# Keys of elements 1 to 7: the seventh block product by a second level of Strassen, and the queries' evicted blocks in the large pool

## The chip, the cores and the metric

The kernel runs on one core of a Trainium2 chip, in one launch. The metric is the device time of that launch in microseconds (us). Its engines are written as in the profile: PE (the matmul engine) with PEld (its weight loads), DVE (vector), ACT (scalar), POOL (GpSimd, here a queue for accumulating DMAs) and SP (a queue for plain DMAs).

## The reference

Two attention layers run over a batch of 8 elements of 512 channels and 32x32 = 1024 tokens, all in float32. Cut to what matters:

```
# layer 0, for each element: x is [1024 tokens, 512]
xn = layer_norm(x) * gamma + beta
q, k, v = xn @ Wq.T + bq, xn @ Wk.T + bk, xn @ Wv.T + bv     # 8 heads of 64
x = softmax(q k^T / 8) v @ Wo.T + bo + x
# layer 1: x is [512, 1024]
h = group_norm(x); q, k, v = wq h + bq, wk h + bk, wv h + bv  # one head of 512
x = x + wp (v softmax(q^T k / sqrt(512))^T) + bp
```

The change touches the projection `k = xn @ Wk.T + bk` of layer 0 for elements 1 to 7, and where the projection `q` of the same elements keeps some evicted blocks.

## The kernel before

A 512x512 weight times a 512x1024 operand is computed as a two by two block product in Strassen's form (Winograd's variant): `STEPS` (line 54) lists seven products of a 256-row weight block or sum of blocks ("11", "12", "S1" to "S4", "22") and an operand block or sum ("11", "21", "22", "T1" to "T4"), with the PSUM bank that each goes to ("x", "y" or "z") and whether it opens that bank. The class `Product` (line 366) runs these steps one at a time: `multiply()` issues the matmuls of a step and `leave()` its eviction. After steps 0, 2 and 3 ACT copies a bank out (`copy`), after steps 1, 4 and 5 DVE adds such a copy and a bank (`out`), after step 6 ACT evicts the last block (`whole`).

For elements 1 to 7 the keys and queries of layer 0 go through `project_deep` (line 589). It takes six of the seven outer products to a second level: each is itself a seven-step `Product` of 128x128 blocks, whose operands are the "deep" sums of a block's quarters. They run as three tandems (`TANDEMS`, line 68), each tandem doing two outer products into the two halves of a bank, so a step is two matmuls of 128x128 weights and 256 columns. The first two tandems run step by step side by side, then the third runs alone. The seventh outer product, weight block "22" times operand "T4", is not taken to the second level: `plain(n)` (line 654) computes it with four matmuls of 128x128 weights and 512 columns, one behind each of the third tandem's steps 0, 1, 3 and 5, in the two banks of the PSUM tile `x0`, and ACT evicts each half with the bias into a tile `m6`. `last()` (line 675) adds `m6` to the other products. The deep sums of the weights were computed and written to DRAM in the first element (`save_deep_later`, line 225), three groups of two for the keys, and `load_deep` reads them back for each element. The deep sums of the operand are made by `deep_operands_later` on DVE, two queue entries for each operand.

What matters for the order: all engines but SP run in the order in which the code is written (`manual_schedule`). Small work is spread over the matmuls by a queue, `side`: `later(...)` appends entries, `tick(n)` pops and runs n of them, and a `Product` calls `tick(self.pieces)` between `multiply()` and `leave()` of each step. Tiles come from pools, in turn: `big` has 46 tiles of 128x1024, `half` 9 tiles of 128x512, PSUM has `ps_s`, 3 tiles of two banks (scores, `x0`, `x1`, `z`), and `ps_a`, two single banks (`bank(...)`).

Element 0 is different. While its queries are projected (lines 1724 to 1731), the queue gets the entries that make the keys' deep weight sums, then the layer norm of element 1 (`ln.queue()`); while its values are projected (from line 1735), the queue also has the deep sums of the other weights. The layer norm's entry puts itself back as second of the queue as long as it has more steps, so it takes turns with the other entries:

```
                    side.insert(len(side) if self.waiting == "now" else 1, piece)
```

Its `variance()` step takes a bank of `ps_a` for two matmuls (`over_channels`, line 1014), and the next step, the first of `root()`, reads that bank with a DVE transpose (line 959). After the values come the scores of the first two pairs of heads, one after the other and with no tick between (`next_scores`, line 1747). In `Pair.scores` (line 1253) block m of a pair is two matmuls of 64 rows that run side by side, mostly into the two banks of a `ps_s` tile that ACT evicts with one exponential; but for three blocks of every two pairs each matmul takes a bank of `ps_a` and has an exponential of its own:

```
                if m + self.c % 2 * NM in (7, 11, 15):
                    s = None
                    parts = [bank(f"s{i}_{self.tag}_{m}") for i in range(2)]
```

Those are block 7 of the first pair and blocks 3 and 7 of the second.

Of the kernel before, what the change touches and what calls it, by code (L numbers as in the profile page):

```python
# [12 lines left out]
F32 = mybir.dt.float32  # L13
I32 = mybir.dt.int32
AF = mybir.ActivationFunctionType
# [5 lines left out]
P = 128  # L21
# [50 lines left out]
def fast_path(ctx: ExitStack, tc: tile.TileContext, x: bass.AP, vecs: dict, weights: dict, out: bass.AP,  # L72
# [13 lines left out]
    nc = tc.nc  # L86
# [18 lines left out]
    def big_tile(name):  # L105
        return big.tile([P, S], F32, tag="b", name=name)

    def half_tile(name):
        return half.tile([P, HB], F32, tag="h", name=name)
# [4 lines left out]
    def bank(name):  # L114
        return ps_a.tile([P, HB], F32, tag="a", name=name)
# [93 lines left out]
            nc.sync.dma_start(out=t, in_=d)  # L209
        return w  # L210

    saved_deep = {n: dram.tile([P, 3, 2, 4, P], F32, tag=f"saved_deep_{n}", name=f"saved_deep_{n}") for n in ("k", "q", "a", "m")}

    def deep_tile(n, b, g):
        return big_tile(f"w_{n}_{b}_{g}_deep").rearrange("p (s i o) -> p s i o", s=2, i=4)

    def load_deep(n, b, groups=range(3), queue=nc.sync):
        ready = {}
        for g in groups:
            deep = deep_tile(n, b, g)  # L220
            queue.dma_start(out=deep, in_=saved_deep[n][:, g])
            ready.update({name: deep[:, k] for k, name in enumerate(SLOTS[2 * g : 2 * g + 2])})
        return ready

    def save_deep_later(n, w, groups=range(3)):

        def sums(g):
            left, right = w[g][:, :, :, :P], w[g][:, :, :, P:]
            made = []

            def one(i, l, r, op):
                if not made:
                    made.append(deep_tile(n, "first", g))
                d = made[0]
                l, r = (d[:, :, x] if isinstance(x, int) else x for x in (l, r))
                nc.vector.tensor_tensor(d[:, :, i], l, r, op)

            later(lambda: one(0, right[:, :, 0], right[:, :, 1], ALU.add),
                  lambda: one(2, left[:, :, 0], right[:, :, 0], ALU.subtract),
                  lambda: one(1, 0, left[:, :, 0], ALU.subtract),  # L240
                  lambda: one(3, left[:, :, 1], 1, ALU.subtract),
                  lambda: nc.gpsimd.dma_start(out=saved_deep[n][:, g], in_=made[0]))

        for g in groups:
            sums(g)
# [340 lines left out]
        for n in names:  # L586
            later(lambda n=n: first(n), lambda n=n: rest(n))

    def project_deep(tag, w, w_deep, bias, h, h_deep, pieces, early):


        made = [[None, None] for _ in TANDEMS]
        wides = {}
        res = {}

        def banks(to, j):
            if to == "y":
                return bank(f"y_{tag}_{j}")
            n = to if to == "z" or j == 2 else f"x{j}"
            if j == 2:  # L600
                return wides["z"][:, :HB] if to == "x" else wides["x1"][:, HB:]
            wides[n] = wides[n] if n in wides else wide_psum(f"{n}_{tag}")
            return wides[n][:, ts(j if to == "z" else 0, HB)]

        def part(dst, a, b, opens):
            for s in range(2):
                nc.tensor.matmul(dst[:, ts(s, CB)], a[s], b[s], start=(opens and s == 0), stop=True,  # L607
                                 skip_group_check=True)

        def view(t):  # L610
            return t.rearrange("p (s t) -> p s t", s=2)

        def unit(j):
            def dest(i, k):
                if made[j][i] is None:
                    made[j][i] = big_tile(f"{tag}_{j}{i}").rearrange("p (s t) -> p s t", s=2)
                return made[j][i][:, :, ts(k, CB)]

            def shift(u, ps, which, add=None):
                if j == 1:  # L620
                    nc.scalar.activation(u, ps, AF.Identity, bias=bias(which[0]))
                else:
                    nc.scalar.copy(u, ps)

            a, b = TANDEMS[j]
            u = Product(f"{tag}_{j}", weight_inner(w, w_deep, a), operand_inner(h, h_deep, b), part, shift, dest,
                        lambda to: banks(to, j))
            u.view = view
            if j < 2 and early:
                for i in range(2):  # L630
                    if j == 0:
                        wides["u", i] = big_tile(f"u{i}1_{tag}")
                    u.loaded[i, 1] = wides["u", i][:, ts(j, HB)]
            return u

        def add(dst, src):
            nc.gpsimd.dma_start(out=dst, in_=src, accum_op=ALU.add)

        def run():
            first, second, third = (unit(j) for j in range(3))  # L640
            for i in range(len(STEPS)):
                first.multiply()
                second.multiply()
                tick(pieces)
                first.leave()
                second.leave()
                yield
            t13, t27, t54 = made
            for r in range(2):
                add(t27[r][:, 0], t13[r][:, 0])  # L650
            until(lambda: "T4" in h)
            rest = {}

            def plain(n):
                r, k = divmod(n, 2)
                ps = wides["x0"]
                nc.tensor.matmul(ps[:, ts(r, HB)], w["22"][:, k, ts(r, P)], h["T4"][:, k, :], start=(k == 0),
                                 stop=(k == 1), skip_group_check=True)
                if k == 1:
                    u = rest[r] = half_tile(f"m6_{tag}_{r}")  # L660
                    nc.scalar.activation(u, ps[:, ts(r, HB)], AF.Identity, bias=bias(2 + r))

            for i in range(len(STEPS)):
                third.step()
                if i in (0, 1, 3, 5):
                    plain((0, 1, 3, 5).index(i))
                if i == 1:
                    for r in range(2):
                        nc.vector.tensor_add(t13[r][:, 1], t13[r][:, 1], t13[r][:, 0])
                        add(t27[r][:, 1], t13[r][:, 1])  # L670
                yield
            for r in range(2):
                add(t27[r][:, 1], t54[r][:, 1])

            def last():
                for r in range(2):
                    nc.vector.tensor_add(t54[r][:, 0], t54[r][:, 0], t13[r][:, 1])
                for r in range(2):
                    nc.vector.tensor_add(lower[r][:, 0], rest[r], t54[r][:, 0])
                for r in range(2):  # L680
                    nc.vector.scalar_tensor_tensor(lower[r][:, 1], t54[r][:, 1], bias(2 + r), t54[r][:, 0], ALU.add,
                                                   ALU.add)

            lower = [big_tile(f"{tag}_lower_{r}").rearrange("p (s t) -> p s t", s=2) for r in range(2)]
            for r in range(2):
                res[r], res[2 + r] = t27[r], lower[r]
            res["last"] = last
            yield
        return run(), res
# [973 lines left out]
    def bias_of(n):  # L1663
        return lambda oc: vec(n, oc)

    with tc.manual_schedule(engines=ORDERED):
# [56 lines left out]

        units, qt = project("q0", wq_now, bias_of("bq0"), hb)
        ln.xt = load_x(1)
        save_deep_later("k", wk_now)
        units[0].step(3)
        ln.queue()
        for u in units:
# [11 lines left out]
        for b in range(B):  # L1741
# [177 lines left out]
                u.finish()  # L1919
            if more:  # L1920
                wk_next = load_w("k", b + 1)
                wk_deep = load_deep("k", b + 1, queue=nc.scalar)
            for u in o_units:
                u.pieces = 2
            o_units[0].rest()
# [1 line left out]
            if not more:  # L1927
                o_units[1].step(1)
            if more:
                deep_operands_later(hb, h_deep, primes_of_h[2:])  # L1930
            o_units[1].rest()
            if more:
                wq_next = load_w("q", b + 1)
                wq_deep = load_deep("q", b + 1)
                steps, kt = project_deep(f"k{b + 1}", wk_next, wk_deep, bias_of("bk0"), hb, h_deep, 2, True)
                for _ in steps:
                    pass
                steps, qt = project_deep(f"q{b + 1}", wq_next, wq_deep, bias_of("bq0"), hb, h_deep, 1, False)
                for n, _ in enumerate(steps):
                    if n == 0:  # L1940
                        kt["last"]()
                    if n == 2 and ln:
                        ln.waiting = False
                qt["last"]()
                vts = {ik: big_tile(f"v{b + 1}_again_{ik[0]}{ik[1]}") for ik in vn_away}
                for ik, d in vn_away.items():
                    nc.sync.dma_start(out=vts[ik], in_=d)
# [384 lines left out]
```

## Time and profile before

| | |
|---|---|
| median of 4 runs | 2790.87 us (2790.64 to 2791.11) |
| the profiled execution | 2789.62 us, of which the span of the core's instructions is 2787.8 us |
| granted PE clock in it | 0.999 |
| busy: PE, PEld | 2777.1, 1628.7 us |
| busy: DVE, ACT, POOL | 2159.2, 1271.4, 521.6 us |
| keys and queries of element 1 in `project_deep` | 419 to 462.5 us of the span |
| first scores of element 0 | 122.66 to 136.66 us |

Busy times are unions of the instructions' spans. A float32 matmul of the program is two MATMUL rows in the trace. The 2789.62 us are 1.25 us under the median of the runs; the sum of the prediction is made as a difference to this execution and carried over to the median.

### The profile page before, as it was taken

The page shows a single profiled execution, that of the slowest core. Times are in us where ns is not written, and L with a number is a line of the kernel's source. Part 1 is how long each engine was busy: PE and PEld are TensorE (multiplying, and loading weights), DVE is VectorE, ACT ScalarE, POOL GpSimd, SP SyncE. Part 2 cuts the span into 40 slices and gives each one's busy share as a digit, 9 for nine tenths or more (in the row PEclk, how much of TensorE's full clock was granted, in tenths as well). Part 3 has the DMA queues.
Part 4 walks back from the last instruction along what each step waited for, and adds up shares of the span by engine and source line. Part 5 has one row for each costly group of instructions (what it writes and reads, how often), then busy time and mean ns, then how long its engine had stood idle before and what let it go on. Part 6 is the DMA issues. An engine that isn't in the chain of part 4 may idle for free.

```text
span 2787.8 us, 32637 instructions
## 1 busy us (share of the span) xinstructions
PE 2777.1 (100%) x11343; PEld 1628.7 (58%) x11343; DVE 2159.2 (77%) x3082; ACT 1271.4 (46%) x2138; POOL 521.6 (19%) x718
## 2 busy tenths in 40 slices
PE   9999999999999999999999999999999999999999
PEld 4535766357553685536854467644676347763375
DVE  6687897778867788777877778778887778857776
ACT  4463435724357242662436534365334743336342
POOL 2031022210222102221022211222012210122001
PEclk9999999999999999999999999999999999999999
DMA  8244467353763547536474364744547434282223
GB/s 317 91 116 126 125 154 193 69 148 102 186 165 70 164 113 195 123 78 186 110 197 102 92 185 114 203 79 113 161 116 208 99 98 132 61 211 63 67 91 96
DMA packets 142462, 370.86 MB, mean 133 GB/s; under 512 B 19936, under 2 KB 24336, under 8 KB 142288
## 3 DMA queue, kind: packets, MB, share of 16 engines
q0 software_dynamic: 58128, 141.08, 27.0%
q1 hardware_dynamic: 81040, 216.56, 22.1%
q10 hardware_dynamic: 3120, 11.04, 1.2%
q8 instruction: 92, 1.51, 0.2%
q14 instruction: 82, 0.67, 0.1%
HBM read 206.59 MB, written 64.49 MB: 97 GB/s over the span
## 4 chain that ended last, share of the span: by engine, by line
PE 99%; DMA 0%; DVE 0%; ACT 0%; issue 0%; SPq 0%; DVEq 0%
PE s L1263 16%; PE acc L1281 16%; PE x_o L509 8%; PE s L1429 7%; PE x_v L493 4%; PE y_o L509 4%; PE x_out L484 4%; PE y_s L1429 3%; PE y_v L493 2%; PE s L1464 2%; PE c_vm L827 2%; PE y_out L484 2%; PE z_o L509 2%; PE x_q L607 2%; PE x_k L607 2%; PE c_qa L701 2%
## 5 line engine op out<-in xcount | busy, mean ns | idle before, releaser
L1272 DVE TENSOR_TENSOR sum<-sum,p 128x1024 f32<-128x1024 f32 x384 | 470.3, 1225 | 40.1 <-ACT p L1266 1.4
L1266 ACT ACTIVATE p<-s 128x1024 f32<-128x1024 f32 (+1 forms) x608 | 478.8, 991 | 15.1 <-PE s L1263 15.1
L1281 PE MATMUL acc<-p,v_again 128*64 128x512 f32 x1792 | 390.9, 594 | 0.0
L1281 PEld LDWEIGHTS acc<-p,v_again 128*64 128x64 f32 x1792 | 126.1, 137 | 261.3 <-issue 236.7
L970 POOL DMA_DIRECT2D fold<-sum x312 | 207.1, 744 | 345.3 <-DMA sum<-sum 212.0
L1263 PE MATMUL s<-q,k 64*128 64x512 f32 x1152 | 252.1, 592 | 0.0
L1263 PE MATMUL s<-q_lower,k_lower 64*128 64x512 f32 x896 | 196.1, 592 | 0.0
L1270 DVE TENSOR_TENSOR sum<-p,p 128x1024 f32<-128x1024 f32 x64 | 78.1, 1220 | 149.4 <-ACT p L1266 149.4
L1263 PEld LDWEIGHTS s<-q,k 64*128 64x128 f32 x1152 | 109.7, 186 | 138.2 <-issue 85.0
L1263 PEld LDWEIGHTS s<-q_lower,k_lower 64*128 64x128 f32 x896 | 85.4, 186 | 110.5 <-issue 68.5
L974 POOL DMA_DIRECT2D sum<-sum x78 | 63.9, 845 | 415.5 <-DVE sum L1272 261.2
L1285 ACT COPY o<-acc 128x512 f32<-128x512 f32 x63 | 36.9, 585 | 221.7 <-PE acc L1281 221.5
L1469 DVE TENSOR_TENSOR p<-p,p 128x1024 f32<-128x1024 f32 x96 | 112.9, 1216 | 6.3 <-ACT p L514 6.3
L509 PE MATMUL x_o<-T_p,S_vm 128*128 128x512 f32 x256 | 114.0, 592 | 0.0
L514 ACT COPY u(0, 0)_v<-x_v 128x512 f32<-128x512 f32 x16 | 9.4, 585 | 186.5 <-PE x_v L493 186.5
L484 PE MATMUL x_out<-T_o,w_o 128*128 128x512 f32 x192 | 89.2, 594 | 0.0
L509 PEld LDWEIGHTS x_o<-T_p,S_vm 128*128 128x128 f32 x256 | 48.6, 190 | 60.8 <-issue 60.8
L1327 ACT COPY rr<-r 32x16 f32<-32x16 f32 x256 | 53.5, 209 | 62.0 <-DVE r L1230 58.6
L493 PE MATMUL x_v<-w_v,T_h 128*128 128x256 f32 x336 | 80.0, 381 | 0.0
L964 DVE STREAM_TRANSPOSE rden<-rr 128x512 f32<-128x512 f32 (+1 forms) x72 | 53.3, 757 | 22.5 <-ACT rr L1572 13.7
L493 PEld LDWEIGHTS x_v<-w_v,T_h 128*128 128x128 f32 x336 | 63.3, 190 | 11.3 <-issue 3.4
L1417 ACT ACTIVATE p<-p 128x1024 f32<-128x1024 f32 x64 | 65.3, 1061 | 0.0
(665 smaller groups left out, 5570.7 us busy)
## 6 DMA issues: line engine op xcount, KB each, us to landing
sum<-sum POOLq DMA_DIRECT2D x78, 256.0 KB, 3.4
fold<-sum POOLq DMA_DIRECT2D x312, 64.0 KB, 2.3
x<-in_x_dram SPq DMA_DIRECT2D x32, 512.0 KB, 6.6
xr<-in_x_dram SPq DMA_DIRECT2D x64, 256.0 KB, 4.2
x_away<-x SPq DMA_DIRECT2D x32, 512.0 KB, 2.8
v_away<-v SPq DMA_DIRECT2D x28, 512.0 KB, 3.0
v_again<-v_away SPq DMA_DIRECT2D x28, 512.0 KB, 9.0
w_o<-saved_o SPq DMA_DIRECT2D x24, 512.0 KB, 5.3
```

The costliest lines, as they stand in the source:

```text
L484: nc.tensor.matmul(dst, a[:, k, ts(r, P)], b[:, k, :], start=(opens and k == 0), stop=(k == 1), skip_group_check=True)
L493: nc.tensor.matmul(dst[:, ts(m, CB)], b[:, k, ts(2 * r + m, P)], a[:, k, :], start=(opens and m == 0 and k == 0), stop=(k == 1), skip_grou ...
L509: nc.tensor.matmul(dst, a[:, r, ts(m, P)], b[m // 2][:, m % 2, :], start=(opens and m == 0), stop=(m == NM // 2 - 1), skip_group_check=True)
L607: nc.tensor.matmul(dst[:, ts(s, CB)], a[s], b[s], start=(opens and s == 0), stop=True, skip_group_check=True)
L970: nc.gpsimd.dma_start(out=f[ts(q + i, BL), :], in_=t[ts(n, BL), ts(i, HB)], accum_op=ALU.add if n else ALU.bypass)
L1263: nc.tensor.matmul(parts[i], self.k[m // 4][r, ts(m % 4, P)], self.q[r, :], start=True, stop=True)
L1266: nc.scalar.activation(dst, src, AF.Exp, scale=1.0 / float(D) ** 0.5)
L1270: nc.vector.tensor_add(self.sum, self.p[0], p)
L1272: nc.vector.tensor_add(self.sum, self.sum, p)
L1281: nc.tensor.matmul(acc[i * D : (i + 1) * D, :], value_of(self.vt, m, self.c * P + i * D, D), self.p[m][:, ts(i, HB)], start=(m == 0), stop ...
L1429: nc.tensor.matmul(dst[:, ts(c, CB)], x[0][:, ts(c, P)], a[0], start=(opens and c == 0), stop=True, skip_group_check=True)
L1469: nc.vector.tensor_add(wide(t), wide(t), wide(x))
```

## The change

Keys: the seventh outer product becomes a `Product` of its own, `sixth`, of seven steps with one matmul of 128x128 weights and 256 columns each. It runs in step with the third tandem, in `x0` (bank "x"), the first bank of `x1` ("z") and a bank of `ps_a` ("y"). Its three copies go to a large tile `u6`, its results to the two tiles `m6`. For that the fourth group of deep weight sums (block "22") is made and saved in element 0 and loaded for each element, and "T4" gets deep sums too. Queries: still with `plain`, but the copies `u(0, 1)` and `u(1, 1)` of the first two tandems are kept in large tiles, as the keys' were (`early`).

```diff
-    saved_deep = {n: dram.tile([P, 3, 2, 4, P], F32, ...
+    saved_deep = {n: dram.tile([P, 4, 2, 4, P], F32, ...
     def load_deep(n, b, groups=range(3), queue=nc.sync):
...
+            names = SLOTS[2 * g : 2 * g + 2]
-            queue.dma_start(out=deep, in_=saved_deep[n][:, g])
+            queue.dma_start(out=deep[:, : len(names)], in_=saved_deep[n][:, g, : len(names)])
...
-    def project_deep(tag, w, w_deep, bias, h, h_deep, pieces, early):
+    def project_deep(tag, w, w_deep, bias, h, h_deep, pieces, early, deep_sixth):
...
+        def sixth_unit(rest):
+            def dest(i, k):
+                if i not in rest:
+                    rest[i] = half_tile(f"m6_{tag}_{i}")
+                return rest[i][:, ts(k, CB)]
+
+            def shift(u, ps, which, add=None):
+                nc.scalar.activation(u, ps, AF.Identity, bias=bias(2 + which[0]))
+
+            def bank_of(to):
+                return bank(f"y6_{tag}")[:, :CB] if to == "y" else wides["x0" if to == "x" else "x1"][:, :CB]
+
+            def narrow(dst, a, x, opens):
+                nc.tensor.matmul(dst, a[0], x[0], start=opens, stop=True, skip_group_check=True)
+
+            u = Product(f"{tag}_6", weight_inner(w, w_deep, ("22",)), operand_inner(h, h_deep, ("T4",)), narrow, shift,
+                        dest, bank_of)
+            u6 = big_tile(f"u6_{tag}")
+            u.loaded = {which: u6[:, ts(n, CB)] for n, which in enumerate(((0, 0), (0, 1), (1, 1)))}
+            return u
...
+            sixth = sixth_unit(rest) if deep_sixth else None
             for i in range(len(STEPS)):
-                third.step()
-                if i in (0, 1, 3, 5):
-                    plain((0, 1, 3, 5).index(i))
+                if sixth:
+                    third.multiply()
+                    sixth.multiply()
+                    tick()
+                    third.leave()
+                    sixth.leave()
+                else:
+                    third.step()
+                    if i in (0, 1, 3, 5):
+                        plain((0, 1, 3, 5).index(i))
...
-        save_deep_later("k", wk_now)
+        save_deep_later("k", wk_now, range(4))
...
-                wk_deep = load_deep("k", b + 1, queue=nc.scalar)
+                wk_deep = load_deep("k", b + 1, range(4), nc.scalar)
...
-                deep_operands_later(hb, h_deep, primes_of_h[2:])
+                deep_operands_later(hb, h_deep, primes_of_h[2:] + ["T4"])
...
-                steps, kt = project_deep(f"k{b + 1}", ..., hb, h_deep, 2, True)
+                steps, kt = project_deep(f"k{b + 1}", ..., hb, h_deep, 2, True, True)
-                steps, qt = project_deep(f"q{b + 1}", ..., hb, h_deep, 1, False)
+                steps, qt = project_deep(f"q{b + 1}", ..., hb, h_deep, 1, True, False)
```

`save_deep_later` makes the same four sums (on one block instead of two) and one store for the fourth group, so it appends five entries more to `side`.

More of the change, by code (lines that the diff above doesn't have):

```diff
@@ L210, in load_w @@
         return w
-    saved_deep = {n: dram.tile([P, 3, 2, 4, P], F32, tag=f"saved_deep_{n}", name=f"saved_deep_{n}") for n in ("k", "q", "a", "m")}
+    saved_deep = {n: dram.tile([P, 4, 2, 4, P], F32, tag=f"saved_deep_{n}", name=f"saved_deep_{n}") for n in ("k", "q", "a", "m")}
     def deep_tile(n, b, g):
@@ L219, in load_deep @@
         for g in groups:
+            names = SLOTS[2 * g : 2 * g + 2]
             deep = deep_tile(n, b, g)
-            queue.dma_start(out=deep, in_=saved_deep[n][:, g])
-            ready.update({name: deep[:, k] for k, name in enumerate(SLOTS[2 * g : 2 * g + 2])})
+            queue.dma_start(out=deep[:, : len(names)], in_=saved_deep[n][:, g, : len(names)])
+            ready.update({name: deep[:, k] for k, name in enumerate(names)})
         return ready
@@ L227, in sums @@
         def sums(g):
-            left, right = w[g][:, :, :, :P], w[g][:, :, :, P:]
+            s = len(SLOTS[2 * g : 2 * g + 2])
+            left, right = w[g][:, :s, :, :P], w[g][:, :s, :, P:]
             made = []
@@ L233, in one @@
                     made.append(deep_tile(n, "first", g))
-                d = made[0]
+                d = made[0][:, :s]
                 l, r = (d[:, :, x] if isinstance(x, int) else x for x in (l, r))
@@ L241, in sums @@
                   lambda: one(3, left[:, :, 1], 1, ALU.subtract),
-                  lambda: nc.gpsimd.dma_start(out=saved_deep[n][:, g], in_=made[0]))
+                  lambda: nc.gpsimd.dma_start(out=saved_deep[n][:, g, :s], in_=made[0][:, :s]))
         for g in groups:
@@ L1934, in fast_path @@
                 wq_deep = load_deep("q", b + 1)
-                steps, kt = project_deep(f"k{b + 1}", wk_next, wk_deep, bias_of("bk0"), hb, h_deep, 2, True)
+                steps, kt = project_deep(f"k{b + 1}", wk_next, wk_deep, bias_of("bk0"), hb, h_deep, 2, True, True)
                 for _ in steps:
                     pass
-                steps, qt = project_deep(f"q{b + 1}", wq_next, wq_deep, bias_of("bq0"), hb, h_deep, 1, False)
+                steps, qt = project_deep(f"q{b + 1}", wq_next, wq_deep, bias_of("bq0"), hb, h_deep, 1, True, False)
                 for n, _ in enumerate(steps):
```

## The prediction

> **What bounds the kernel now.** I read the page's busy times and the chain that ended last, then PE's waits, to see whether anything but PE's own work has a price.
>
> ```profile
> PE 2777.1 (100%) x11343; PEld 1628.7 (58%) x11343; DVE 2159.2 (77%) x3082; ACT 1271.4 (46%) x2138; POOL 521.6 (19%) x718
> PE 99%; DMA 0%; DVE 0%; ACT 0%; issue 0%; SPq 0%; DVEq 0%
> ```
>
> The waits of PE, complete:
>
> ```profile
> PE pst_k L304 <- DMA w_k<-in_L_conv_wk_dram: 1.9, 1, 1.9
> PE ps_first L1669 <- DVE checks L142: 1.3, 1, 1.3
> PE pm L1203 <- DVE mv L1197: 0.6, 1, 0.6
> PE x_qa L484 <- DVE gn L1225: 0.4, 1, 0.4
> PE psw_a L315 <- ACT nat_k L307: 0.2, 1, 0.2
> PE pst_q L304 <- DMA w_q<-in_L_conv_wq_dram: 0.2, 1, 0.2
> ```
>
> PE is the chain from end to end, and it waits 4.6 us in all, none of it in the stages the change touches. So a PE column taken away is time gained, a new PE wait is time lost, and nothing later can win it back. Three places decide. The first is PE's timeline at the start of the keys' third tandem (start, length, what; a length runs to the modelled end of the last matmul of the line):
>
> ```profile
> 431.38 1.03 PE L607 MATMUL z_k<-T_h,w_k 128*128 128x256 f32 x4
> 432.24 1.02 PE L657 MATMUL x_k<-T_h,w_k 128*128 128x512 f32 x2
> 433.10 1.03 PE L607 MATMUL x_k<-T_h,w_k 128*128 128x256 f32 x4
> 433.96 1.02 PE L657 MATMUL x_k<-T_h,w_k 128*128 128x512 f32 x2
> ```
>
> One plain matmul (two rows of 512 columns) holds PE for 433.10 - 432.24 = 0.86 us; a step of the tandem (two matmuls of 256 columns, four rows) also 0.86, so one narrow matmul takes 0.43. The second is ACT's timeline in the same stage, where two evictions must be out before PE may reuse their bank:
>
> ```profile
> 431.58 0.69 ACT L621 ACTIVATE k<-x_k,vecs 128x512 f32<-128x512 f32 x1 [0.28 <-PE x_k L607]
> 441.05 0.58 ACT L623 COPY k<-z_k 128x512 f32<-128x512 f32 x1 [0.17 <-PE z_k L607]
> ```
>
> The third is element 0: the layer norm's variance bank, its transpose, and the first scores. The lines are from the timelines of PE, DVE and ACT, the last one being ACT's answer for the instant about 130 us.
>
> ```profile
> 112.82 1.08 PE L1014 MATMUL var<-lnq,ones_c 128*64 128x512 f32 x4
> 113.97 0.72 DVE L959 STREAM_TRANSPOSE vart<-var 128x512 f32<-128x512 f32 x1 [0.29 <-PE var L1014]
> 122.66 14.00 PE L1263 MATMUL s<-q,k 64*128 64x512 f32 x64
> 123.84 14.96 ACT L1266 ACTIVATE p<-s 128x1024 f32<-128x1024 f32 x19 [0.48 <-PE s L1263]
> 129.28 1.57 ACT L1266 ACTIVATE p<-s 128x1024 f32<-128x1024 f32 x2
> ```
>
> Before, the bank is free 1.9 us after it was taken, and 8 us before the scores. The 16 score blocks then run without a break: 0.86 us each on PE, 0.90 on ACT, which falls slowly behind.
>
> **Part 1, the seventh product: a gain.** Removed for each element: 4 x 0.86 = 3.44 us of PE. Added: 7 x 0.43 = 3.03 (by the chain of waits, where eight rows of 256 columns take 1.73: 14 x 0.216). That is -0.41 an element, -2.9 us over seven. The Trainium skill's page "TensorE: Matmul & The Clock Gate", section "Back-to-back issue gap", speaks against it: it gives a sustained spacing of 81 ns for 128 columns and 131 ns for 512, so a narrow matmul would cost more for each column. Read off halfway, about 98 ns for 256 columns (an estimate from that page), eight wide rows would become 14 narrow ones at 1.05 against 1.37 us, and the part would lose 2.3 us. The trace has 0.43 and 0.216 us for the two widths, exactly proportional, and I go by it.
>
> **What is added beside PE, at nothing.** DVE: three deep sums of "T4" (0.68 + 0.42 + 0.42 by lines 577, 581 and 582) and three adds of 128x256 from PSUM; no row has that shape, 0.42 is the row of 128x256 in SBUF and 0.69 the row of 128x512 from PSUM, I take 0.42. Together 2.8 us an element. From 419 to 441 us DVE is busy 12.2 of 22 us, which covers it. ACT: four evictions of 128x256 in the place of two of 0.69; between nothing less than 0.3 and 0.69 each, I take 0.45, so +0.4 us, beside 8.8 busy of 22. One load more of 256 KB on ACT's queue, with one issue of 0.44 us at about 400 us, where ACT next sits idle 2.1 us. Its bytes share the DMA engines (281 GB/s from 419 to 441, so 0.9 us of them). Who would feel it is the queries' deep weights: last issued at 426.4, median landing 12.2, first used at 444.3, 5.7 us to spare. If all that cover were gone, each late microsecond there would cost one on PE. The queries' two copies in large tiles change an address and no instruction: nothing, between -0.1 and +0.1 an element, since ACT waits for no tile there.
>
> **Two covers get thinner.** Step 1 of the tandem waits for the ACT line at 431.58, out at 432.27. Its weight load must start one row before its matmul: 432.67 before, 432.46 with 0.43 in the place of 0.86. About 0.15 us is left with the semaphore's 0.04. At the end, the built order of the changed program lets the queries' second matmul wait for the k<-z_k copy: it is out 1.65 us after the last tandem step starts, and the weight load comes 0.86 + 0.43 + 0.86 - 0.22 = 1.93 after, so 0.25 is left. I take no cost; it is the slow rival.
>
> **Part 2, five entries more in the queue of element 0: a loss.** The four sums and the store stand in `side` ahead of the layer norm's first entry: 17 entries instead of 12 after the first three steps. At two ticks a step the layer norm starts 2.5 steps later in the queries' 11 remaining steps. There it had the queue to itself and ran two pieces a step; it loses five pieces, and in the values' stage, where it takes turns with other weights' sums, it makes up none. Five steps later than at 112.82 (1.73 us each) is the last step of the values. The built order of the changed program says the same: the two variance matmuls stand directly behind the last values matmul, and the transpose that reads them stands on DVE behind all 14 sum additions of the first two pairs, because no tick lies between. So one of the two `ps_a` banks is held through both pairs' scores, and in each of the three split blocks the second matmul must take the first one's bank, after its exponential; the program's waits say so too.
>
> First split block (block 7). The 64 rows end at 136.66, so the last block starts at 136.66 - 0.59 - 0.43 = 135.64 and block 7 at 135.64 - 8 x 0.858 = 128.78. The first half's exponential ends at 129.28 + 1.57 = 130.85. With a hand-over of 0.25 (weight load 0.19, matmul behind it 0.02, semaphore 0.04) the second matmul starts at 131.10 instead of 128.78, and it still needs its 0.86: +2.32. ACT has caught up by then: an exponential starts 0.43 + 0.59 + 0.04 = 1.06 behind its block's start, and three wide blocks later 3 x 0.045 more, 1.19. A half exponential takes 0.62 (1.03 unhurried for a wide one, less 0.41 between the wide and half rows) to 0.71 (its mean row there). So the second and third split block cost 1.19 + 0.66 + 0.25 = 2.1 each. Sum +6.5. Bounds: a hand-over of 0.2 to 0.5 (the longest ACT wait for a score) and 0.6 to 0.74 for the half give 6.2 to 7.4. The late transposes and scalings of the layer norm (about 7 us of DVE) then meet 27 us of value matmuls and further scores and hurry nobody; if that cover failed, `ln.done` would be late at the third pair.
>
> **Sum.** -2.9 + 6.5 = +3.6 us on the profiled 2789.62: 2793.2, and on the median 2790.87 + 3.6 = 2794.5. That is 0.13%; 0.2% (5.6 us) is about what a measurement of this kernel can tell from no change.
>
> **Rivals.** *No stall*: if the bank came free before block 7 after all, only part 1 is left, 2788.0. For it: before, the transpose follows within 0.3 us. Against: it is issued behind sums that need the exponentials of both pairs. Chance 0.07. *Slower*: the thin covers in the keys. If ACT's evictions come out over 0.15 us later at the first place and over 0.25 at the second, PE pays the rest in each element; with ACT 0.35 us late at both, 0.2 + 0.1, times seven, +2.1, and with 0.5 late +4.2, so 2796.6 to 2798.7. It decides from 0.35 late on. For it: ACT gains a second eviction a step and one DMA issue. Against: it sits idle before both lines (0.28 and 0.17). Chance 0.11. *The narrow matmul is not half a wide one*: 0.43 would have to be 0.49 to eat the gain, 2797.4; the rows exclude it nearly. Chance 0.02. My case has 0.80.
>
> **How the numbers follow.** My case spans 2793 to 2796 with the bounds above. The range 2791.0 to 2797.5 takes it in, with part of the slow rivals; the no-stall case stays outside. Faster by over 0.2% (under 2785.3) needs twice the whole gain of part 1: 0.02. Slower by over 0.2% (over 2796.5): most of the two slow rivals, 0.12. Within: 0.86.
>
> **What would show it.** PE's waits after: a new line of about 6.5 us over three times, s L1294 for ACT p L1297, near 130 to 145 us, the variance matmuls just ahead of the scores and their transpose some 15 us later. In the keys' third tandem of every element, seven pairs of a tandem step and a narrow matmul 1.29 apart, with no idle time; the period from element to element shorter by 0.41. Wrong would be: a score stage as smooth as before, or PE waiting for ACT k in elements 1 to 7.

## The result, and the profile after

The changed kernel takes 2794.02 us (median of 39 runs, 2792.66 to 2795.92) against 2790.51 us before (59 runs): +3.5 us, a ratio of 1.0014 with a 95% interval of 1.0009 to 1.0018. The forecast was +3.6 us, 2794.5.

The profiled execution of the changed kernel took 2793.61 us, with a span of 2791.9. The page's line of busy times:

```profile
PE 2776.4 (99%) x11385; PEld 1637.1 (59%) x11385; DVE 2176.7 (78%) x3128; ACT 1273.8 (46%) x2152; POOL 522.7 (19%) x719
```

All PE waits (line waited for: us in total, times, longest):

```profile
PE s L1294 <- ACT p L1297: 4.5, 3, 1.7
PE pst_k L306 <- DMA w_k<-in_L_conv_wk_dram: 1.9, 1, 1.9
PE ps_first L1700 <- DVE checks L142: 1.3, 1, 1.3
PE pm L1234 <- DVE mv L1228: 0.6, 1, 0.6
PE pst_q L306 <- DMA w_q<-in_L_conv_wq_dram: 0.5, 1, 0.5
PE x_qa L486 <- DVE gn L1256: 0.4, 1, 0.4
PE psw_a L317 <- ACT nat_k L309: 0.2, 1, 0.2
```

The first wait is new, three times, at the line that was announced; nothing waits for the keys' evictions. PE's timeline of element 0 shows where (start, length, then the wait ahead of the row group):

```profile
122.72 1.08 PE L1045 MATMUL var<-lnq,ones_c 128*64 128x512 f32 x4
123.73 7.13 PE L1294 MATMUL s<-q,k 64*128 64x512 f32 x30
131.97 3.70 PE L1294 MATMUL s<-q,k 64*128 64x512 f32 x16 [1.11 <-ACT p L1297]
137.38 3.70 PE L1294 MATMUL s<-q,k 64*128 64x512 f32 x16 [1.71 <-ACT p L1297]
142.80 1.12 PE L1294 MATMUL s<-q,k 64*128 64x512 f32 x2 [1.71 <-ACT p L1297]
```

The variance matmuls stand directly ahead of the scores, and the scores stop after 30, 46 and 62 of their 64 rows: each time behind the first matmul of a split block. DVE's timeline shows what holds the other bank, ACT's (the last line) what frees the one that PE takes instead:

```profile
126.88 1.23 DVE L1301 TENSOR_TENSOR sum<-p,p 128x1024 f32<-128x1024 f32 x1 [4.75 <-ACT p L1297]
144.59 1.22 DVE L1303 TENSOR_TENSOR sum<-sum,p 128x1024 f32<-128x1024 f32 x1 [0.20 <-ACT p L1297]
145.73 0.71 DVE L990 STREAM_TRANSPOSE vart<-var 128x512 f32<-128x512 f32 x1
124.91 7.01 ACT L1297 ACTIVATE p<-s 128x1024 f32<-128x1024 f32 x8 [1.49 <-PE s L1294]
```

The transpose that frees the variance's bank runs at 145.73, 22 us after the bank was filled, behind the sums of both pairs. Before, it ran at 113.97. The eight exponentials of the ACT line are the seven blocks ahead of the first split block and that block's first half; they end at 131.92, and PE goes on at 131.97.

Now the keys' third tandem of element 1, in PE's and ACT's timelines:

```profile
438.63 1.03 PE L609 MATMUL z_k<-T_h,w_k 128*128 128x256 f32 x4
439.50 0.59 PE L654 MATMUL x_k<-T_h,w_k 128*128 128x256 f32 x2
439.93 1.03 PE L609 MATMUL x_k<-T_h,w_k 128*128 128x256 f32 x4
440.79 0.59 PE L654 MATMUL x_k<-T_h,w_k 128*128 128x256 f32 x2
441.22 1.03 PE L609 MATMUL z_k<-T_deep_h,w_k_deep 128*128 128x256 f32 x4
438.83 0.69 ACT L623 ACTIVATE k<-x_k,vecs 128x512 f32<-128x512 f32 x1 [0.28 <-PE x_k L609]
440.18 0.48 ACT L648 ACTIVATE u_k<-x_k,vecs 128x256 f32<-128x256 f32 x1
```

A pair of a tandem step and a narrow matmul takes 439.93 - 438.63 = 1.30 us, of which the narrow one is 0.43, with no idle time.

**Where the 4.1 us between the two spans are.** The start times of the same matmuls in the two traces were subtracted. The difference is +1.07 us when the scores of element 0 begin, +7.26 when they end, and falls by 0.42 in each element's keys, to +4.14 at the end. So the scores cost 6.19, the keys give back 7 x 0.42 = 2.94 (0.2 more goes in small pieces elsewhere), and 1.07 arose ahead of everything that the change touches. Most of that part is the arrival of an input:

```profile
17.91 1.23 DVE L1050 TENSOR_TENSOR lns<-x,x 128x1024 f32<-128x1024 f32 x1 [2.25 <-DMA x<-in_x_dram]
19.91 0.19 PEld L1045 LDWEIGHTS mean<-lns,ones_c 128*64 128x64 f32 x2 [0.71 <-DVE lns L1054]
```

In the trace of before the same DVE instruction started at 16.59, and PE's four rows of `mean` took 1.08 us instead of 1.97. Without it the two traces differ by 3.1, the medians by 3.5.

### The profile page after: what moved, and what is told of

Same layout as the page of the kernel before. It is cut to its first block, busy times and chain, and to the rows that moved or that the text cites. A ratio compares the mean times of both kernels' runs of the same rounds, so it can differ in the third digit from the quotient of the medians.

```text
span 2791.9 us, 32794 instructions
## 1 busy us (share of the span) xinstructions
PE 2776.4 (99%) x11385; PEld 1637.1 (59%) x11385; DVE 2176.7 (78%) x3128; ACT 1273.8 (46%) x2152; POOL 522.7 (19%) x719
## 4 chain that ended last, share of the span: by engine, by line
PE 99%; ACT 0%; DMA 0%; DVE 0%; issue 0%; SPq 0%; DVEq 0%
PE acc L1312 16%; PE s L1294 16%; PE x_o L511 8%; PE s L1460 7%; PE x_v L495 4%; PE y_o L511 4%; PE x_out L486 4%; PE y_s L1460 3%; PE y_v L495 2%; PE s L1495 2%; PE c_vm L858 2%; PE y_out L486 2%; PE z_o L511 2%; PE x_q L609 2%; PE x_k L609 2%; PE c_qa L732 2%
```

## Experiments

Differences are of medians, against the kernel before as run beside them (2790.83 for the first four, 2790.78 for the next four). Theory A is the prediction's: the five entries push the variance to the end of the values, its bank is held through two pairs of scores, and the split blocks need both banks.

**The fourth group's sums made later.** Part 1 alone.

```diff
-        save_deep_later("k", wk_now, range(4))
+        save_deep_later("k", wk_now)
...
         save_deep_later("m", wm, (1, 2))
+        save_deep_later("k", wk_now, (3,))
```

> The changed kernel with the fourth group's five entries appended after all the others, in the values' stage, instead of ahead of the layer norm. Theory A (the bank of the variance is held through the first two pairs' scores, because the five entries push the variance to the end of the values; part 1 is a gain): the three waits of s L1294 for ACT p L1297 are gone and only part 1 is left, -2.9 us against the kernel before (seven times -0.42), about 2787.6. Rival B (the loss has nothing to do with where the entries stand; it comes with the extra deep group, its load, or the large tiles): the waits stay and the time is +3.5 as in the changed kernel.

Measured: 2787.84 us, -3.0 (ratio 0.9990, 0.9981 to 0.9999). The variance is back in the middle of the values, and the 64 rows of scores run in one piece:

```profile
113.20 1.08 PE L1045 MATMUL var<-lnq,ones_c 128*64 128x512 f32 x4
114.21 1.99 PE L495 MATMUL x_v<-w_v_first,T_h 128*128 128x256 f32 x8
123.04 14.00 PE L1294 MATMUL s<-q,k 64*128 64x512 f32 x64
```

Theory A holds, rival B falls: the same extra sums, loads and tiles cost nothing when the entries stand elsewhere.

**Only the fourth group's sums, on the kernel before.** Part 2 alone: `save_deep_later` and `saved_deep` of the changed kernel, and one call.

```diff
-        save_deep_later("k", wk_now)
+        save_deep_later("k", wk_now, range(4))
```

> The kernel before, which also makes and saves the fourth group's deep sums, ahead of the layer norm as in the changed kernel; nothing reads what it saves, the keys' seventh product and the queries' tiles stay as before. Theory A: the whole loss and no gain, +6.2 to +6.5 us against the kernel before (2796.7 to 2797.0), with three waits of s L1294 for ACT p L1297 at 130 to 145 us. Rival B: the loss belongs to the deep seventh product or to the large tiles, so nothing here, 2790.5, no such wait.

Measured: 2797.73 us, +6.9 (1.0024, 1.0015 to 1.0034). The same three waits, in a kernel whose keys are untouched:

```profile
PE s L1264 <- ACT p L1267: 4.5, 3, 1.7
```

So the change is the sum of two parts of opposite sign. The 6.9 lies a little over the expected 6.2 to 6.5. Counted by start times, this kernel's trace loses 6.4 in the scores and 1.4 more in the matmuls of the values behind them; the last experiment looks at the second loss.

**Two entries run ahead of the scores.** The layer norm stays late, only its transpose moves ahead of the sums.

```diff
             u.pieces = 2
             u.rest()
+        tick(2)
         for b in range(B):
```

> The changed kernel with two entries of the queue run between the values and the first scores of element 0, so that the transpose that frees the variance's bank stands on DVE ahead of the sum additions; the layer norm is as late as in the changed kernel (variance directly behind the values). Theory A: the bank is free about 2 us into the scores, before block 7, no wait, -2.9 us against the kernel before, 2787.6. Rival C (the lateness of the layer norm is what costs, by its work colliding with the scores): most of the +6.2 stays, the time is +2 to +3.5 against the kernel before.

Measured: 2787.41 us, -3.4 (0.9988, 0.9979 to 0.9997). PE's and DVE's timelines:

```profile
122.50 1.08 PE L1045 MATMUL var<-lnq,ones_c 128*64 128x512 f32 x4
123.51 14.00 PE L1294 MATMUL s<-q,k 64*128 64x512 f32 x64
123.63 0.72 DVE L990 STREAM_TRANSPOSE vart<-var 128x512 f32<-128x512 f32 x1 [1.72 <-PE var L1045]
126.66 1.23 DVE L1301 TENSOR_TENSOR sum<-p,p 128x1024 f32<-128x1024 f32 x1 [2.01 <-ACT p L1297]
```

The variance is where it was in the changed kernel, right ahead of the scores, and the whole loss is gone: the bank is free at 124.4. Rival C, that a late layer norm costs by itself, falls.

**Four entries instead of five.** The fourth group's last sum and its store in one entry; no instruction more or less.

```diff
+            if g == 3:
+                work[3:] = [lambda two=work[3:]: [f() for f in two]]
+            later(*work)
```

> The changed kernel with the fourth group's last sum and its store in one entry of the queue: the same instructions, four entries more instead of five. Theory A says there is a cliff: the variance then comes one step before the last of the values, its transpose is run by that step's tick, ahead of the sum additions, and the whole loss goes at once: -2.9 us against the kernel before, 2787.6. Rival C (cost in proportion to the delay): four fifths of 6.2 stay, +2.1 against the kernel before, 2792.6.

Measured: 2787.99 us, -2.8 (0.9990, 0.9980 to 0.9999).

```profile
121.59 1.08 PE L1048 MATMUL var<-lnq,ones_c 128*64 128x512 f32 x4
122.60 1.99 PE L498 MATMUL x_v<-w_v_first,T_h 128*128 128x256 f32 x8
122.75 0.72 DVE L993 STREAM_TRANSPOSE vart<-var 128x512 f32<-128x512 f32 x1 [0.36 <-PE var L1048]
124.53 14.00 PE L1297 MATMUL s<-q,k 64*128 64x512 f32 x64
```

One step of the values is still left behind the variance, its tick runs the transpose, and nothing is lost. It is a cliff: the fifth entry costs all 6 us, the first four nothing.

**No split block in the first two pairs.** The bank stays held, but nobody asks for two.

```diff
+            self.first = b == 0 and hf == 0 and c < 2
...
-                if m + self.c % 2 * NM in (7, 11, 15):
+                if m + self.c % 2 * NM in (7, 11, 15) and not self.first:
```

> The changed kernel, in which the first two pairs of element 0 have no split block: all 16 blocks go through the three two-bank tiles, each with one exponential. The variance's bank is held as long as in the changed kernel. Theory A (the loss needs both, a held bank and blocks that ask for two of them): no wait of 1 to 2 us, the scores run at ACT's 0.90 us a block at the slowest, which over 16 blocks is at most 16 x 0.045 = 0.7 us behind PE; so -2.9 to -2.2 against the kernel before, 2787.6 to 2788.3. Rival C (the late layer norm itself disturbs the scores): +2 to +3.5 against the kernel before.

Measured: 2787.79 us, -3.0 (0.9989, 0.9980 to 0.9998).

```profile
123.16 14.38 PE L1295 MATMUL s<-q,k 64*128 64x512 f32 x64
144.54 0.71 DVE L990 STREAM_TRANSPOSE vart<-var 128x512 f32<-128x512 f32 x1
```

The transpose is as late as in the changed kernel, and the scores take only 14.38 - 14.00 = 0.38 us more. Both halves of the mechanism are needed.

**Only the queries' copies in large tiles, on the kernel before.**

```diff
-                steps, qt = project_deep(f"q{b + 1}", ..., hb, h_deep, 1, False)
+                steps, qt = project_deep(f"q{b + 1}", ..., hb, h_deep, 1, True)
```

> The kernel before with one edit: the queries' copies u(0, 1) and u(1, 1) of the first two tandems in large tiles. The prediction put this at nothing, between -0.1 and +0.1 us an element: 2790.5 within 0.7 us. Theory B (the tiles' turn shifts a wait somewhere): a difference of over 1 us, with a new line among PE's waits.

Measured: 2790.64 us, -0.1 (1.0000, 0.9991 to 1.0009), no new wait. An edit costed at nothing that cost nothing.

**How thin is the first cover?** On the kernel with two entries run ahead of the scores, copies on ACT between two evictions of the keys make the second one late: four copies, then two.

```diff
                 first.leave()
+                if deep_sixth and i == len(STEPS) - 1:
+                    for _ in range(4):
+                        nc.scalar.copy(ones, ones)
                 second.leave()
```

> The changed kernel with the two entries run ahead of the scores, and with four copies of a 128x128 tile onto itself on ACT between the two evictions of the first two tandems' last step, in each of elements 1 to 7: it makes ACT late by a known amount at the first of the two thin covers. A copy is taken as 0.2 to 0.25 us, so the eviction k<-x_k comes 4 x 0.2 (or 0.25) - 0.28 = 0.5 to 0.7 us later; the prediction left a cover of 0.15 us there, so PE should wait 0.35 to 0.6 us in each element, 2.4 to 4 us in all, in a new line of PE's waits for ACT k. Rival D (the cover is thicker than worked out): no such line, same time as without the copies (-3.4 against the kernel before).

> As the kernel with four copies, with two: the eviction comes 2 x 0.2 (or 0.25) - 0.28 = 0.1 to 0.2 us later, about the cover of 0.15: PE waits 0 to 0.1 us an element, 0 to 0.5 in all, and the time stays at -3.4 to -2.9 against the kernel before. Rival D: nothing at all; were there no cover, 0.2 an element, 1.4.

Measured: 2791.35 us with four copies, +3.9 against 2787.41 without them; 2787.49 with two, +0.1. ACT's and PE's timelines with four:

```profile
431.27 0.59 ACT L625 COPY k<-x_k 128x512 f32<-128x512 f32 x1 [3.63 <-PE x_k L609]
431.76 1.29 ACT L671 COPY ones<-ones 128x128 f32<-128x128 f32 x4
432.95 0.68 ACT L623 ACTIVATE k<-x_k,vecs 128x512 f32<-128x512 f32 x1
432.80 0.59 PE L654 MATMUL x_k<-T_h,w_k 128*128 128x256 f32 x2
433.69 1.13 PE L609 MATMUL x_k<-T_h,w_k 128*128 128x256 f32 x4 [0.29 <-ACT k L623]
434.65 0.59 PE L654 MATMUL x_k<-T_h,w_k 128*128 128x256 f32 x2
```

PE's new wait (total, times, longest):

```profile
PE x_k L609 <- ACT k L623: 2.0, 7, 0.3
```

Without copies the eviction starts 0.86 us behind the copy ahead of it, here 432.95 - 431.27 = 1.68: it is 0.82 late. PE's step starts 433.69 - 432.80 = 0.89 behind the narrow matmul instead of 0.43, and the next one 0.96 instead of 0.86: 0.46 + 0.10 = 0.56 us an element, 3.9 over seven, which is the measured difference. With two copies the eviction is 0.16 late (1.02 - 0.86) and no such wait is in the trace. So the cover is at least 0.16 us, rather than 0.15, and 0.82 - 0.56 = 0.26 if each microsecond beyond it costs one, which two points can't tell. Rival D falls with four copies: the cover is thin. A copy took 0.27 to 0.30 us, more than the 0.2 to 0.25 taken.

**The changed kernel again, three traces.**

> The changed kernel once more, for a second trace. Its 39 runs lie in two groups, about 2793.5 and 2795.3 us. In the trace of the before kernel with only the fourth group saved, the first four steps of the values behind the last split block stand 0.85 to 0.9 us apart instead of 0.43 (1.6 us in all); in the trace of the changed kernel none does. Theory E (behind the stall the two 64-column matmuls of a step sometimes restart one after the other instead of side by side): a run of the upper group shows such steps behind 143 us, a run of the lower one shows none; the stall itself is 6.2 us in both. Rival F (the groups are the scatter of the input loads at the start): the steps are 0.43 apart in both, and the difference stands ahead of 25 us.

> The changed kernel, third trace; expected as for the second.

> The changed kernel, fourth trace; expected as for the second.

Measured: 2792.88, 2794.44 and 2793.47 us. PE waits 4.5 us for ACT p in each of the three traces; only in the second do the values behind the scores go out of step. PEld's timeline of that run (start, length, then the idle time before), and PE's line for the 64 rows of both pairs' values:

```profile
142.44 0.30 PEld L1312 LDWEIGHTS acc<-p,v 128*64 128x64 f32 x4 [0.76 <-issue]
143.35 0.23 PEld L1312 LDWEIGHTS acc<-p,v 128*64 128x64 f32 x2 [0.61 <-issue]
144.20 0.23 PEld L1312 LDWEIGHTS acc<-p,v 128*64 128x64 f32 x2 [0.62 <-issue]
145.06 0.23 PEld L1312 LDWEIGHTS acc<-p,v 128*64 128x64 f32 x2 [0.62 <-issue]
145.89 0.14 PEld L1312 LDWEIGHTS acc<-p,v 128*64 128x64 f32 x2 [0.60 <-issue]
146.32 0.14 PEld L1312 LDWEIGHTS acc<-p,v 128*64 128x64 f32 x2 [0.29 <-issue]
142.44 15.64 PE L1312 MATMUL acc<-p,v 128*64 128x512 f32 x64
```

For four steps the weight loads are about 0.85 us apart instead of 0.43; then they fall into step. The 64 rows take 15.64 us, 1.7 more than the 13.95 of the trace of before. Theory E holds for this run. It has a share of rival F too: up to 25 us it is 1.4 us ahead of the first trace of the changed kernel, so that without the late steps it would have been about as fast as the fastest of the four. Late steps (0.91, 0.85 and 0.86 us, 1.4 in all) are in the trace of the fourth group alone, too: two of five traces with the stall have them, none of the eight without it. That this makes the two groups among the 39 runs is argued from these, not shown run by run.

## Why the prediction was right

- **What bounds the kernel: right.** PE is busy 2776.4 of 2791.9 us. What PE lost at 130 to 143 us stands in the final time, and so does what it saved in the keys.
- **Part 1, -0.41 an element: right.** The trace has -0.42; -2.9 was forecast, and the four kernels that keep part 1 and lose the stall without adding to the keys measure -3.0, -3.4, -2.8 and -3.0. The narrow row is proportional: a narrow matmul takes 0.43 us, a wide one took 0.86. The estimate worked out from the Trainium skill's page "TensorE: Matmul & The Clock Gate", section "Back-to-back issue gap", would have made this part a loss of 2.3 us; for these float32 rows the measurement decides against it. (Its 98 ns for 256 columns is a third of the way between the two figures, as 256 is between 128 and 512, and not halfway.)
- **What was put beside PE: right.** DVE is busy 14.68 of the 22 us from 426.25 to 448.25, the stretch that matches 419 to 441 of before (12.2 + 2.8 = 15.0 was forecast), ACT 9.35 (9.2). An eviction of 128x256 from PSUM took 0.48 on ACT (0.45 taken), an add 0.41 on DVE (0.42). The large tiles: nothing.
- **Part 2, the mechanism: right in each link.** Variance directly behind the values, transpose behind the sums, three waits at the split blocks. Each link was cut alone: the entries, the tick, the last entry, the split blocks. Each cut regains the whole 6 us.
- **Part 2, the size: 6.5 forecast, 6.19 in the trace,** just under the lower bound of 6.2. The mis-sized term is the first stall, 2.32: counted by the starts of equal rows it is 1.70, then 1.98 and 1.98 for the two taken at 2.1, and 0.53 at the end. The working was off there in two places. It put the hand-over from the exponential to the second matmul at 0.25 us, and PE's row starts 0.05 behind the exponential's end (131.92 to 131.97). And it let the delayed second matmul run its 0.86 us alone: it runs beside the first matmul of the next block, as the row counts of 30, 16, 16 and 2 show, so only the last one is without a partner. That the total came within 0.1 us of the forecast is in part luck: the keys and the scores alone give 6.19 - 2.94 = +3.25, and the medians have +3.5. The steps out of phase behind the stall, 1.4 and 1.7 us in the two traces that have them, were not in the prediction and can make up the rest; that they do is not shown.
- **The slow rival: rightly kept, its threshold near.** The cover was put at 0.15 us and is 0.16 or a little more. An eviction 0.82 late cost 0.56, which is one for one beyond 0.26, or 0.85 for one beyond 0.16. In the changed kernel ACT was not late, so it was not paid. The second cover, 0.25 us at the queries' second matmul, was not tried.
- **What would show it: as written, but for two numbers.** The transpose came 23 us behind the variance matmuls (122.72 to 145.73) and not some 15. At 15 the bank would have been free before the third split block asked for it, so the 15 didn't agree with the prediction's own order, in which the transpose waits for all 14 sums. And the wait view says 4.5 us where 6.5 was announced and 6.19 was lost. It counts from a row's modelled end, 0.59 us after its start, while rows in a stream follow each other every 0.43; and it sees neither the rows that run without a partner nor the 0.10 us by which the first row behind a stall is slower. With four copies on ACT it says 2.0 for a loss of 3.9.
- **What a measurement can tell: finer than written.** The 0.2% of the prediction was too coarse; with 39 and 59 runs a difference of 0.14% has an interval of 0.09 to 0.18%.

The version to keep is the changed kernel with the two entries run ahead of the scores (2787.41 us) or with the group's sums later (2787.84); between the two no run can tell. Both are faster than the kernel before and the changed kernel; against the kernel before, the intervals of the ratio (0.9979 to 0.9997 and 0.9981 to 0.9999) end just under 1. The queries' seventh product at the second level was not tried.

## What to carry to other kernels

Work that goes into a shared queue costs by what it pushes back, not by its own time: five small entries that DVE had room for moved a PSUM bank's reader behind the next stage's work, and that was worth twice the gain of the change. Look in the built order for the last reader of each bank ahead of a stage that has no ticks, and count how many entries are left before it falls behind; here it was four. Take the price of a stall from start times, since the wait view gave half to three quarters of it.

## What the runs showed of the hardware

- **Two matmuls of 64 columns that share PE can restart out of phase.** Behind a stall three or four of the steps that follow took 0.83 to 0.91 us instead of 0.43 in two of five traces; four of the five are of one program, and one of those has them.
- **The inputs' arrival moves the start by a good part of an edit's gain.** The sum that waits for the load of x began at 16.59 us in one trace and 17.91 in another; PE's four rows of `mean` took from 1.08 to 2.39 us in the traces, and the wait view of PE shows 0.2 us of it at most: it stands as a wait of PEld inside a row group that counts as busy. Two traces that differ by 1 us in the span need their starts compared first.
- **The first of two thin covers held with the eviction 0.16 us late and cost 0.56 us an element with it 0.82 late.** At one for one, an eviction about 0.7 us late (0.26 + 0.42, an estimate from these) would have eaten the whole gain of part 1.
